# Four graph layers in one kernel: layer 0's second attention pass with the decoder's work placed between the next part's blocks, and its last 20 keys held in three copies

## The chip, the cores and the metric

The program runs on one core of one Trainium2 chip, as one launch that computes all four layers. The metric is the time on the device in microseconds (us); smaller is better. The core has five engines that work side by side, each in the order of its own queue: TensorE (PE in the profile; its weight loads are listed as PEld), VectorE (DVE), ScalarE (ACT), GpSimd (POOL) and SyncE (SP). They wait for each other by semaphores. SBUF is the memory on the chip, with 128 partitions; PSUM holds the sums of TensorE in 8 banks of 512 float32 columns for each partition.

## The reference

There are N = 2708 nodes with 512 features, and one 0/1 adjacency `adj` of 2708 x 2708 (about 1.2% of it is set). Layer 0 is the one the change touches. It is called with `adj` as the local and as the long-range pattern, so that its two softmaxes are the same one.

```python
H, D = 4, 128
Xh = X.reshape(n, H, D).transpose(1, 0, 2)
Xw = jnp.einsum('hnd,hde->hne', Xh, W)
f1 = jnp.einsum('hnd,hd->hn', Xw, V[:, 0, :, 0])
f2 = jnp.einsum('hnd,hd->hn', Xw, V[:, 1, :, 0])
sig = jax.nn.sigmoid(f1[:, :, None] + f2[:, None, :])
att = _masked_softmax(adj[None] * sig, (adj != 0)[None])
Xa = jnp.einsum('hij,hjd->hid', att, Xw)
Xc = Xa.transpose(1, 0, 2).reshape(n, F)
Xn = _batchnorm(Xc, enc_bn_gamma, enc_bn_beta)
emb = _mlp_block(Xn, enc_mlp_W, ...)          # batchnorm(elu(x @ Wm.T + bm) + x)
Yh = emb.reshape(n, H, D).transpose(1, 0, 2)
Y = jnp.einsum('hij,hjd->hid', att, Yh)       # the second pass
Y = jnp.einsum('hnd,hed->hne', Y, W)          # the decoder: w0T
Yc = jax.nn.elu(Y.transpose(1, 0, 2).reshape(n, F))
out = _mlp_block(Yc, dec_mlp_W, ...)          # dec_w, elu, + x, batchnorm
```

The layer's output is added to its input and normalised by rows. Layers 1 to 3 (a mean over neighbours, and two softmax layers over all pairs) follow; the change leaves them as they are.

## The kernel before

Everything is float32. Layer 0 works on transposed data: features on the partitions, nodes along the columns. It runs over the keys twice. The first pass (`attention_pass(xw, True, ..., keep)`) gives `Xa` and the softmax's sums, the second (`attention_pass(emb, False, ..., decode)`) gives `Y` with the same weights, which are computed again.

A pass has four parts: the queries in two halves of 1354 (`hf`), and for each half two pairs of heads (`p`). A part runs over 22 blocks of keys (`BLOCKS`): 21 of 128 and a last one of 20, since 2708 = 21 x 128 + 20. For each block `form` makes a tile `t` of weights, 128 keys x (2 heads x 1354 queries): SP loads a stripe `a` of the adjacency (L300), ACT takes tanh for each of the two heads (L313), DVE multiplies with the stripe (L321), ACT takes exp of both (L322). Four tiles `t` go round. Some blocks' tiles (`KEPT`) are written to DRAM in the first pass and loaded back in the second. In the first pass's parts with `p` = 0 the stripe is first prepared by DVE (L303, L304) and written to DRAM for later (L307, POOL). L284 counts neighbours for layer 1.

TensorE then multiplies the tile with the block's values (L366): two heads x three chunks of 452, 452 and 450 queries (`HCH`), six products a block, added up over all 22 blocks in six PSUM banks `po` (three tiles `both[q]` of two banks). Of the last block, the products have 20 rows. In the first pass there are also the softmax's sums (L389, four 32-column products side by side).

When a part is through, `finish` is called. In the first pass it is `keep`: it copies the six banks to `ft` (L466), computes a small product once (`ps_beta`, L434), and returns the scaling by the sums as a list `later`, of which one entry is done with every block after the fourth (`jt > 3`). In the second pass it is `decode`, which does its whole work at once. It reads the six banks with scaling (L660, into `ot`), and for each of the six chunks adds a shift where a node has neighbours (L672), multiplies with w0T (`ps_y`, L676) and takes elu (L403 on ACT, L406 and L408 on DVE). After the second pair of heads of a half follows the decoder's mlp: for each of three chunks and four output blocks, four products with `dec_w` (`ps_dec`, L687), elu (L405 on ACT), the addition to `ot` (L705) and statistics for the batch normalisation (L706). `ps_y` and `ps_dec` share two more banks (`misc`).

After the second pass, layer 1's weights are loaded and centred (L735, L737), the statistics are put together (L418) and inverted (`inv_std`: L92, a square root on ACT at L93, L94), and layer 1 starts with scaling `ot` (L774), adding the input (L781) and transposing (L787) and multiplying (L113) each block of nodes. The order of instructions in each engine's queue is fixed when the program is built, by a scheduler that follows the order of the code where it can.

Of the kernel before, what the change touches and what calls it, by code (L numbers as in the profile page):

```python
# [17 lines left out]
P = 128  # L18
# [11 lines left out]
def gnn_stack_kernel(  # L30
# [32 lines left out]
    BANK = 512  # L63

# [86 lines left out]
    with ExitStack() as l0:  # L151
# [20 lines left out]
        f2h = p0.tile([P, NT, H], F32, name="f2h")  # L172

# [12 lines left out]
        def project(att, psum):  # L186
# [41 lines left out]
            for jt, (j0, n) in enumerate(BLOCKS):  # L228
                pxw = psum.tile([P, H // HP, BANK], F32, tag=f"po{jt % HB}", name="pxw")
                pv = pxw[:, :, : HP * (P + 2)].rearrange("p a (k e) -> p a k e", k=HP)  # L230
                for h in range(H):
                    nc.tensor.matmul(
                        pv[:n, h // HP, h % HP, :],
                        xT_sb[:, h, j0 : j0 + n],
                        w0x[:, h, :],
                        start=True,
                        stop=True,
                    )
                copy = nc.vector.tensor_copy if jt % 3 == 2 else nc.scalar.copy
                copy(  # L240
                    xw[:n, jt, :].rearrange("p (a k d) -> p a k d", a=H // HP, k=HP),
                    pv[:n, :, :, :P],
                )
                nc.vector.tensor_scalar(
                    f2h[:n, jt, :].rearrange("p (a k) -> p a k", k=HP),
                    pv[:n, :, :, P + 1],
                    0.5,
                    None,
                    ALU.mult,
                )  # L250
            return f1b
# [18 lines left out]
        def attention_pass(values, first, att, psum, finish, f1b=None):  # L270
# [23 lines left out]
            def form(hf, p, jt, att, prepare, f1b, tv):  # L294
# [5 lines left out]
                nc.sync.dma_start(a[:n, :w], src[j0 : j0 + n, h0 : h0 + w])  # L300
                if prepare:
# [5 lines left out]
                    nc.gpsimd.dma_start(adj_d[j0 : j0 + n, h0 : h0 + w], a[:n, :w])  # L307
# [16 lines left out]
            later = []  # L324
            for hf, (h0, w) in enumerate(HSPAN):
                for p in range(H // HP):
                    prepare = first and p == 0
                    if f1b is None or not prepare or hf > 0:
# [6 lines left out]
                    both = [  # L335
                        psum.tile([P, HP, BANK], F32, tag=f"po{q}", name="po", bufs=1)
                        for q in range(HB)
                    ]
                    po = [both[q][:, k, :] for k in range(HP) for q in range(HB)]
# [7 lines left out]
                    for jt, (j0, n) in enumerate(BLOCKS):  # L347


                        if jt > 3 and later:  # L350
                            later.pop(0)()
# [3 lines left out]
                        if kept is None or first:  # L355
                            form(hf, p, jt, att, prepare, f1b, tv)
                            if kept is not None:
                                nc.gpsimd.dma_start(kept[:n, :, :w], tv)
                        else:
                            nc.sync.dma_start(tv, kept[:n, :, :w])  # L360
                            if p == 0 and jt in KEPT[1]:
                                count(hf, jt, att)
                        for k in range(HP):
                            h = HP * p + k
                            for q, (q0, qw) in enumerate(HCH[hf]):
                                nc.tensor.matmul(  # L366
                                    po[HB * k + q][:, :qw],
                                    values[:n, jt, h * P : (h + 1) * P],
                                    t[:n, k, q0 : q0 + qw],
                                    start=(jt == 0),  # L370
                                    stop=(jt == NT - 1),
                                )
# [23 lines left out]
                    later += finish(hf, p, po, sums if first else rb) or []  # L396

        def elu(pool, ps, w, bias=None, less=-1.0, dst=None):
# [5 lines left out]
            else:  # L404
                nc.scalar.activation(m, ps, AF.Exp, bias=bias)  # L405
            nc.vector.tensor_scalar(r, ps, less, -1.0, ALU.add, ALU.max)  # L406
# [39 lines left out]
        with (  # L446
# [7 lines left out]
            def keep(hf, p, po, sums):  # L454
# [3 lines left out]
                elif hf == 0 and p == 1:  # L458
                    ps = psum.tile([P, HP, BANK], F32, tag="po0", name="ps_beta")[:, 0, :C]
                    small_product(ps, mlp_w[0], prm_sb[:, B_ENC, :])  # L460
                    nc.vector.tensor_tensor(bias[:, 0, :], ps, prm_sb[:, MB_ENC, :], ALU.add)
                final = hf == NHALF - 1 and p == H // HP - 1
                for k in range(HP):
                    for q, (q0, qw) in enumerate(HCH[hf]):
# [3 lines left out]
                        )  # L468
                sm = [att.tile([P, BW], F32, tag="rs", name="sm") for _ in range(HP)]
# [86 lines left out]
        with (  # L556
# [36 lines left out]
            for ci, (c0, w) in enumerate(CHUNKS):  # L593
# [34 lines left out]
                while turned < NT and sum(BLOCKS[turned]) <= c0 + w:  # L628
# [5 lines left out]
                    turned += 1  # L634

# [8 lines left out]
            links = {}  # L644

            def decode(hf, p, po, rb):
# [10 lines left out]
                for k in range(HP):  # L657
                    h = HP * p + k
                    for q, (q0, qw) in enumerate(HCH[hf]):
                        nc.vector.scalar_tensor_tensor(  # L660
                            t[:, h, q0 : q0 + qw],
                            po[HB * k + q][:, :qw],
                            scale2[:, h : h + 1],
                            rb[:, k, q0 : q0 + qw],
                            ALU.mult,
                            ALU.mult,
                        )
                for k in range(HP):
                    h = HP * p + k
                    for q, (q0, qw) in enumerate(HCH[hf]):  # L670
                        y = t[:, h, q0 : q0 + qw]
                        nc.vector.scalar_tensor_tensor(  # L672
                            y, y, shift2[:, h : h + 1], linked[:, q0 : q0 + qw], ALU.add, ALU.mult
                        )
                        ps = psum.tile([P, BANK], F32, tag="misc", name="ps_y", bufs=2)
                        nc.tensor.matmul(  # L676
                            ps[:, :qw], w0T_sb[:, h, :], y, start=True, stop=True
                        )
                        elu(att, ps[:, :qw], qw, dst=y)
                if p + 1 < H // HP:  # L680
                    return
                for q, (q0, qw) in enumerate(HCH[hf]):
                    rs = []
                    for o in range(C):
                        ps = psum.tile([P, BANK], F32, tag="misc", name="ps_dec", bufs=2)
                        for c in range(C):
                            nc.tensor.matmul(  # L687
                                ps[:, :qw],
                                dec_w[:, c, o * P : (o + 1) * P],
                                t[:, c, q0 : q0 + qw],  # L690
                                start=(c == 0),
                                stop=(c == C - 1),
                            )
                        rs.append(
                            elu(
                                att,
                                ps[:, :qw],
                                qw,
                                prm_sb[:, MB_DEC, o : o + 1],
                                bm1[:, o : o + 1],  # L700
                            )
                        )
                    for o in range(C):
                        dst = t[:, o, q0 : q0 + qw]
                        nc.vector.tensor_tensor(dst, dst, rs[o], ALU.add)  # L705
                        nc.vector.bn_stats(stats[:, o, HB * hf + q, :], dst)  # L706

# [164 lines left out]


    Q = 32
    REST = N - NFULL * P
    assert 0 < REST <= Q and C * Q == P
# [538 lines left out]
```

## Time and profile before

The median of three timed runs is 3387.1 us (3385.58 to 3390.83). The profiled execution took 3383.28 us; the span from its first to its last instruction is 3381.5 us.

| stretch, us from the span's start | what runs |
|---|---|
| 0 to 592 | projections and the first pass; parts end at about 183, 312, 457 and 584 |
| 592 to 703 | weights of a later layer, the encoder's mlp |
| 703 to 1181 | the second pass; parts end at about 812, 921, 1074 and 1181 |
| 921 to 974 | the decoder's mlp of the first half, with first blocks of the third part |
| 1181 to 1231 | the decoder of the last part |
| 1231 to 1244 | until layer 1's first transpose |
| 1244 to 3381 | layers 1 to 3 |

| group | count | mean ns of one |
|---|---|---|
| L313 ACT, tanh of one head | 324 | 1414 |
| L322 ACT, exp of both heads | 162 | 2452 |
| L321 DVE, product with the stripe | 162 | 2975 |
| L366 PE, 128 keys x 452 queries (second pass) | 672 | 556 |
| L366 PE, 20 keys x 452 queries (second pass) | 32 | 550 |

How to read it: a float32 matmul stands in the profile as two records. Matmuls overlap their neighbours, so the mean of one is longer than the step from one to the next. The rows of the windows view give, for each engine, busy time and (xN) the number of its records, then the granted TensorE clock, the share of the DMA engines and GB/s. Square brackets in a timeline give idle time before a row, and what ended it.

### The profile page before, as it was taken

How to read it: one execution, taken by the hardware profiler on the slowest of the kernel's cores; microseconds unless marked ns; L12 is line 12 of the kernel's file. 1: busy time of each engine (PE TensorE's matmuls, PEld its weight loads, DVE VectorE, ACT ScalarE, POOL GpSimd, SP SyncE). 2: the span in 40 equal slices, each digit the busy share in tenths (PEclk: the TensorE clock that was granted, in tenths of full speed). 3: DMA queues.
4: the chain of work that ended last, by engine and by line, in shares of the span. 5: the costliest groups of instructions: out<-in, count | busy, mean ns of one | idle time of the engine just before them, and what ended most of it. 6: DMA issues, size and time to landing. Idle time of an engine off the chain costs nothing.

```text
span 3381.5 us, 30504 instructions
## 1 busy us (share of the span) xinstructions
PE 3304.0 (98%) x10981; PEld 1761.1 (52%) x10981; DVE 1988.8 (59%) x3227; ACT 1339.6 (40%) x1491; POOL 127.6 (4%) x205
## 2 busy tenths in 40 slices
PE   8999999999999989999999999999999999999998
PEld 4444444544444445886555555444455555555554
DVE  7867977767687585445136666777253442543533
ACT  6877887568858743001133333333011010110110
POOL 1100100000000000000010000000000000000001
PEclk9998999999999999999999999999999999999999
DMA  7655753335524331550034444554111111111100
GB/s 279 246 164 166 276 184 114 120 103 168 184 82 160 126 106 61 140 136 19 0 114 125 116 127 128 145 148 112 58 50 35 44 33 44 37 33 44 35 23 19
DMA packets 167483, 364.03 MB, mean 108 GB/s; under 512 B 20374, under 2 KB 111194, under 8 KB 164100
## 3 DMA queue, kind: packets, MB, share of 16 engines
q1 hardware_dynamic: 152596, 298.43, 29.3%
q0 software_dynamic: 14736, 63.66, 5.0%
q8 instruction: 86, 1.41, 0.2%
q14 instruction: 65, 0.53, 0.0%
HBM read 298.34 MB, written 63.35 MB: 107 GB/s over the span
## 4 chain that ended last, share of the span: by engine, by line
PE 74%; issue 15%; DVE 6%; DMA 2%; ACT 2%; POOL 1%; SPq 0%; POOLq 0%; DVEq 0%; ACTq 0%
PE po L1090 22%; PE ps_s L996 17%; PE po L366 8%; PE ps_nb L842 7%; PE ps_wide L908 4%; PE ps_hid L113 2%; PE ps_sup L1233 2%; DVE t L321 2%; PE ps_o L1168 2%; PE ps_dec L687 2%; PE ps_mlp L601 1%; DMA a<-adj_d 1%; POOL adj_d L307 1%; PE ps_s L991 1%; ACT t L313 1%
## 5 line engine op out<-in xcount | busy, mean ns | idle before, releaser
L321 DVE SCALAR_TENSOR_TENSOR t<-t,a 128x2708 f32<-128x2708 f32 (+1 forms) x162 | 479.3, 2975 | 144.8 <-ACT t L313 143.3
L313 ACT ACTIVATE t<-f1b,f2h 128x1354 f32<-128x1354 f32 (+1 forms) x324 | 445.3, 1414 | 91.2 <-PE psm L389 47.1
L366 PE MATMUL po<-t,xw 128*128 128x452 f32 (+3 forms) x1056 | 433.0, 561 | 3.9 <-ACT t L322 3.9
L366 PE MATMUL po<-t,emb 128*128 128x452 f32 (+3 forms) x1056 | 416.3, 552 | 10.7 <-ACT t L322 9.2
L322 ACT ACTIVATE t<-t 128x2708 f32<-128x2708 f32 (+1 forms) x162 | 396.7, 2452 | 52.0 <-DVE t L321 50.5
L1090 PE MATMUL po<-sup,e 128*128 128x512 f32 x882 | 410.0, 601 | 5.2 <-DVE e L1277 5.2
L1090 PE MATMUL po<-e,xs 128*128 128x384 f32 (+1 forms) x1176 | 407.5, 489 | 0.0
L996 PE MATMUL ps_s<-q,hT 128*128 128x384 f32 (+1 forms) x1176 | 403.5, 489 | 0.0
L1331 DVE SCALAR_TENSOR_TENSOR e<-a_cols,ps_s 128x384 f32<-128x384 f32 (+1 forms) x154 | 85.6, 556 | 419.7 <-PE ps_s L996 396.6
L366 PEld LDWEIGHTS po<-t,emb 128*128 128x128 f32 (+1 forms) x1056 | 201.6, 193 | 220.1 <-issue 199.2
L366 PEld LDWEIGHTS po<-t,xw 128*128 128x128 f32 (+1 forms) x1056 | 197.8, 193 | 224.9 <-issue 211.4
L996 PEld LDWEIGHTS ps_s<-q,hT 128*128 128x128 f32 x1176 | 222.6, 190 | 161.5 <-issue 6.2
L1090 PEld LDWEIGHTS po<-e,xs 128*128 128x128 f32 x1176 | 221.6, 190 | 157.2 <-issue 6.0
L1090 PEld LDWEIGHTS po<-sup,e 128*128 128x128 f32 x882 | 162.0, 192 | 176.8 <-issue 148.3
L996 PE MATMUL ps_s<-hT 128*128 128x384 f32 (+1 forms) x672 | 229.2, 488 | 1.0 <-ACT sup L1240 0.7
L93 ACT ACTIVATE ln_rstd<-ln_rstd 128x1 f32<-128x1 f32 x88 | 17.2, 201 | 497.4 <-DVE ln_rstd L92 496.9
L1273 ACT ACTIVATE a_cols<-a_cols,neg_big 128x384 f32<-128x384 f32 (+1 forms) x154 | 94.8, 616 | 249.7 <-DMA a_cols<-in_adjT_dram 208.4
L842 PE MATMUL ps_nb<-hid_hi,at 128*128 128x512 f32 x484 | 188.1, 390 | 0.4 <-DVE at L836 0.4
L842 PE MATMUL ps_nb<-hid_lo,at 128*128 128x512 f32 x484 | 187.8, 389 | 0.0
L1067 ACT COPY nmax<-pb 128x384 f32<-128x384 f32 (+1 forms) x14 | 6.7, 479 | 430.5 <-PE pb L1054 349.8
L996 PEld LDWEIGHTS ps_s<-hT 128*128 128x128 f32 x672 | 125.8, 190 | 97.1 <-issue 18.0
L1085 DVE TENSOR_TENSOR acc<-acc,e 128x384 f32<-128x384 f32 (+2 forms) x294 | 162.9, 554 | 12.3 <-ACT e L1075 2.3
(223 smaller groups left out, 3474.1 us busy)
## 6 DMA issues: line engine op xcount, KB each, us to landing
a<-adj_d SPq DMA_DIRECT2D x116, 677.0 KB
a_cols<-in_adjT_dram SPq DMA_DIRECT2D x378, 192.0 KB
a<-in_adjT_dram SPq DMA_DIRECT2D x42, 677.0 KB
adj_d<-a POOLq DMA_DIRECT2D x42, 677.0 KB, 4.5
raw<-in_adjT_dram SPq DMA_DIRECT2D x105, 256.0 KB
kept<-t POOLq DMA_DIRECT2D x10, 1354.0 KB, 6.6
t<-kept SPq DMA_DIRECT2D x10, 1354.0 KB
a_cols<-in_adjT_dram SPq DMA_DIRECT2D x63, 202.0 KB
```

Source lines behind the costliest of these rows:

```text
L113: nc.tensor.matmul(ps[:n], xt[:, c, :n], w[:, c, :], start=(c == 0), stop=(c == C - 1))
L313: nc.scalar.activation(tv[:, k, :], f1b[:n, k, :w], AF.Tanh, bias=f2h[:n, jt, h : h + 1], scale=0.5,)
L321: nc.vector.scalar_tensor_tensor(tv, tv, GUARD, ab, ALU.add, ALU.mult)
L322: nc.scalar.activation(tv, tv, AF.Exp, scale=0.5)
L366: nc.tensor.matmul(po[HB * k + q][:, :qw], values[:n, jt, h * P : (h + 1) * P], t[:n, k, q0 : q0 + qw], start=(jt == 0), stop=(jt == NT - 1),)
L842: nc.tensor.matmul(pos[it], at, half[:, jt, :], start=(jt == 0 and k == 0), stop=(jt == NT - 1 and k == 1),)
L908: nc.tensor.matmul(ps[:, :width], w(c, o), xt(c), start=(c == 0), stop=(c == C - 1),)
L996: nc.tensor.matmul(ps[:, :w], keys[:, c, j0 : j0 + P], st["q"][:, c, :], start=(c == 0), stop=(c == C - 1),)
L1085: nc.vector.tensor_tensor(acc, acc, e[:m], ALU.add)
L1090: nc.tensor.matmul(out, lhsT, rhs, start=(k == 0), stop=(k == NT - 1))
L1273: nc.scalar.activation(a, a, AF.Identity, bias=neg_big[: a.shape[0]], scale=1.0e30)
L1331: nc.vector.scalar_tensor_tensor(e, a, 2.0, ps, ALU.mult, ALU.add)
```

## The change

Three things, all in layer 0.

*Twenty keys in three copies.* The values of the last block, and f2 of its nodes, are copied by POOL to the rows 32 to 51 and 64 to 83 (`copies`). The last block's stripe `a` is loaded three times, to rows 0, 32 and 64; the 12 rows between are filled from other rows of the adjacency. `form` works on 84 rows (`HR`), and the products of chunk q take the rows from 32 q. Kept tiles are loaded three times.

*Banks.* The six banks are allocated once for each pass instead of for each part; `ps_beta` uses the first of them, after the copies.

*The decoder.* `decode` still reads the six banks when a part ends. Shift, product with w0T and elu of each chunk (`after`), and the mlp of the chunks 0 and 1 of the first half, are returned as a list; one entry is done with every block from the second on. The mlp of the first half's chunk 2 is kept in `spare` and done behind the last block of the second pass, where the last part's work is written out by chunk. There (`wide`) the mlp's result goes to a tile `r` of its own, so that it can be added and its statistics taken at once; ACT copies three of four back. A square root of one column (`ready`) comes before the last statistics.

```diff
+        def copies(rows):
+            for r in range(1, HB):
+                nc.gpsimd.dma_start(rows[r * Q : r * Q + REST], rows[:REST])
...
+            copies(xw[:, NT - 1, :])
+            copies(f2h[:, NT - 1, :])
...
                 nc.sync.dma_start(a[:n, :w], src[j0 : j0 + n, h0 : h0 + w])
+                if n < P:
+                    for r in range(HB):
+                        if r > 0:
+                            nc.sync.dma_start(
+                                a[r * Q : r * Q + n, :w], src[j0 : j0 + n, h0 : h0 + w]
+                            )
+                        if r + 1 < HB:
+                            nc.sync.dma_start(
+                                a[r * Q + n : (r + 1) * Q, :w], src[: Q - n, h0 : h0 + w]
+                            )
+                    n = HR
...
-                        if jt > 3 and later:
+                        if jt > (3 if first else 0) and later:
                             later.pop(0)()
...
-                            nc.sync.dma_start(tv, kept[:n, :, :w])
+                            for r in range(0, P if n == P else HB * Q, P if n == P else Q):
+                                nc.sync.dma_start(t[r : r + n, :, :w], kept[:n, :, :w])
...
                             for q, (q0, qw) in enumerate(HCH[hf]):
+                                r = 0 if n == P else q * Q
                                 nc.tensor.matmul(
                                     po[HB * k + q][:, :qw],
-                                    values[:n, jt, h * P : (h + 1) * P],
-                                    t[:n, k, q0 : q0 + qw],
+                                    values[r : r + n, jt, h * P : (h + 1) * P],
+                                    t[r : r + n, k, q0 : q0 + qw],
...
+            if last:
+                ready = small.tile([P, 1], F32, tag="ready", name="ready")
+                nc.scalar.activation(ready, m[:, 0:1], AF.Sqrt)
...
+                def after(k, q):
+                    shifted(k, q)
+                    turn(k, q)
+
+                if not final:
+                    for k in range(HP):
+                        for q in range(HB):
+                            take(k, q)
+                    rest = [lambda k=k, q=q: after(k, q) for k in range(HP) for q in range(HB)]
+                    for q in range(HB if last else 0):
+                        st = {}
+                        wide = q + 1 == HB
+                        dest = spare if wide else rest
+                        dest += [
+                            lambda q=q, o=o, st=st, wide=wide: mlp(q, o, st, wide) for o in range(C)
+                        ]
+                    return rest
+
+                def begin(q):
+                    for k in range(HP):
+                        take(k, q)
+                    for k in range(HP):
+                        shifted(k, q)
+
+                def turns(q):
+                    for k in range(HP):
+                        turn(k, q)
+
+                begin(0)
+                spare[0]()
+                turns(0)
+                spare[1]()
+                begin(1)
+                spare[2]()
+                spare[3]()
+                for q in range(HB):
+                    st = {}
+                    mlp(q, 0, st, True)
+                    mlp(q, 1, st, True)
+                    if q + 1 < HB:
+                        turns(q + 1)
+                    if q + 2 < HB:
+                        begin(q + 2)
+                    mlp(q, 2, st, True)
+                    mlp(q, 3, st, True)
```

`take` is the read of one bank (the old L660), `shifted` the old L672, `turn` the old L676 with its elu. `mlp(q, o, st, wide)` holds the four products and the elu of one output block:

```python
                def mlp(q, o, st, wide):
                    ...
                    r = None
                    if wide:
                        if o == 0:
                            st["r"] = att.tile([P, HP, HW], F32, tag="t", name="r_dec", bufs=4)
                        r = st["r"].rearrange("p k w -> p (k w)")[:, o * BW : o * BW + qw]
                    r = elu(att, ps[:, :qw], qw, ..., dst=r, last=final and q + 1 == HB and o + 1 == C)
                    st.setdefault("sums", []).append((t[:, o, q0 : q0 + qw], r, o))

                    def add(dst, y, r, o):
                        nc.vector.tensor_tensor(dst, y, r, ALU.add)
                        nc.vector.bn_stats(stats[:, o, HB * hf + q, :], dst)

                    if wide and o + 1 < C:
                        y, r, o = st["sums"][-1]
                        add(r, y, r, o)
                    elif o + 1 == C:
                        for y, r, o in st["sums"]:
                            if wide and o + 1 < C:
                                nc.scalar.copy(y, r)
                            else:
                                add(y, y, r, o)
```

## The prediction, made before the changed kernel was run

> **What bounds the kernel now.** I read the page first, then the stretch that the change touches part by part, then single instructions. All times are of the profiled execution: 3383.3 us, span 3381.5.
>
> ```profile
> PE 3304.0 (98%) x10981; PEld 1761.1 (52%) x10981; DVE 1988.8 (59%) x3227; ACT 1339.6 (40%) x1491; POOL 127.6 (4%) x205
> PEclk9998999999999999999999999999999999999999
> PE 74%; issue 15%; DVE 6%; DMA 2%; ACT 2%; POOL 1%; SPq 0%; POOLq 0%; DVEq 0%; ACTq 0%
> ```
>
> TensorE sets the time, so an edit is worth what it takes from TensorE's queue or from TensorE's waits. A busy PE is not PE at its peak, however. The chain of waits, in order of time, has one undisturbed stretch:
>
> ```profile
> 828.08 77.62 PE po L366 x204
> ```
>
> 77.62 / 204 = 0.38 us is one record of 452 columns at full clock; each float32 matmul makes two. Below, records x 0.38 is "work", and the rest of a stretch is "excess". The two passes over the keys end at about 592 and 1181 us; each has four parts (two halves of the queries, two pairs of heads). The second pass, cut where a part's last matmul ends:
>
> ```profile
> core 0: us, PE busy (x) PEld busy (x) DVE busy (x) ACT busy (x) POOL busy (x), PEclk, DMA share, GB/s
> 812.50:921.60 109.10, 107.27 (x277) 52.63 (x276) 74.99 (x54) 95.81 (x62) 0.00 (x0) 0.98 0.54 179
> 921.60:974.00 52.40, 51.09 (x128) 24.80 (x129) 48.91 (x71) 21.94 (x24) 0.00 (x0) 0.97 0.30 101
> 974.00:1074.90 100.90, 95.84 (x246) 46.31 (x244) 74.48 (x57) 84.78 (x52) 0.00 (x0) 0.98 0.39 123
> 1074.90:1181.60 106.70, 106.66 (x276) 52.73 (x276) 63.96 (x47) 81.35 (x53) 0.00 (x0) 0.98 0.42 142
> 1181.60:1231.00 49.40, 44.06 (x109) 20.71 (x109) 35.85 (x62) 10.28 (x17) 0.00 (x0) 0.94 0.32 115
> 1231.00:1244.00 13.00, 3.60 (x9) 1.36 (x8) 11.97 (x30) 3.69 (x6) 0.00 (x0) 0.81 0.58 184
> ```
>
> Excess, row by row: 109.1 - 277 x 0.38 = 3.8; 52.4 - 48.6 = 3.8; 100.9 - 93.5 = 7.4; 106.7 - 104.9 = 1.8; 49.4 - 41.4 = 8.0. The last row is the wait for the batch statistics: TensorE leaves its last decoder product at 1231.0 and starts layer 1 at 1244.0. In row 2 VectorE is busy 48.91 of 52.40 us.
>
> **1. Twenty keys in three copies.** Groups by shape, and the same kind of product later in the kernel, where 20-row matmuls already sit in different row groups:
>
> ```profile
> L366 PE MATMUL po<-t,emb 20*128 20x452 f32 x32 | 13.8, 550 | 0.0
> 2013.62 1.13 PE L1090 MATMUL po<-values,e 20*128 20x512 f32 x6
> ```
>
> Now a 20-key block is 12 records in single file, 12 x 0.38 = 4.57 us. At L1090 six records of 512 columns take 1.07 us to the next start (2013.62 to 2014.69): three run at once, in two rounds. The changed block is two such groups of 452 columns: 2 x 1.07 x 452/512 = 1.9 us. Saved: 2.7 us x 8 blocks = **21.3 us**. Bounds: 0 (no overlap) to 8 x (4.57 - 4 x 0.38) = 24.4.
>
> [...]
>
> What it adds elsewhere: ACT and DVE work on 84 rows for 20, at no cost, since the time goes by columns: the 20-row L321 at 572.08 us took 2.97, the mean of the group is 2975 ns. SP issues four more loads at the end of each of the first pass's parts, two more in the second's; at 0.5 us (three L300 issues took 1.50) that is 2 us of SP per part, with the next part's first loads queued behind. The four `a` buffers of the first pass hide it; uncovered it would be 8 us. POOL issues six more copies, 0.57 us each (an L507 issue) and 3.4 in all, with `adj_d` writes behind them that are read a part later: nothing.
>
> **2. What the short block uncovers.** The six reads of the sums were under the 4.57 us:
>
> ```profile
> 811.10 3.66 DVE L660 SCALAR_TENSOR_TENSOR ot<-po,bn_scale,rb 128x452 f32<-128x452 f32 x6 [1.26 <-PE po L366]
> 814.68 3.08 DVE L672 SCALAR_TENSOR_TENSOR ot<-ot,bn_shift,linked 128x452 f32<-128x452 f32 x5
> 822.57 2.97 DVE L321 SCALAR_TENSOR_TENSOR t<-t,a 128x2708 f32<-128x2708 f32 x1
> ```
>
> Two reads (2 x 0.6, and 0.2 of signalling) must be done before the next part's first product; before, TensorE waited 0.1 there. So 1.4 us at each of the three inner ends of each pass: 8.4. In the second pass DVE now does one shift, then an L321, then the second shift, and TensorE's queue has both `ps_y` products after the part's first block. From the block's end DVE needs 3.7 (six reads) + 0.6 + 3.0 + 0.6 = 7.9 us, TensorE 1.4 + 4.57 + 0.76 = 6.7: a wait of 1.1, three times, with all later `po` products behind it. Given back: **11.7 us**. Bounds: 0 (banks free one by one as they are summed) to twice that. Allocating the banks once adds no instruction; I give it nothing.
>
> **3. Decoder work spread out.** 48 products of dec_w per half and 6 `ps_y` per part stay. Half 0's 12 x 4 products no longer stand at the part's start: 8 x 4 go between blocks of the third part, 4 x 4 behind the last block. VectorE still does for a part's six turns 6 x (0.6 + 1.15) = 10.5 us, and per dec step about 2.3 us (0.6 + 0.54 + 0.54 + 0.6) under 3.04 of products. In the third part: 19 L321 (56) + 20 L284 (31, at 1.55) + reads 4.2 + 10.5 + 8 x 2.3 = 120 us. TensorE has 21 blocks of 4.57 and one of 1.9, the six turns and 32 products: 97.9 + 4.6 + 24.3 = 127. That is tight, so of row 3's 7.4 I take back only 2.9. Of row 2's 3.8, 1.7 is clock (below), 2.1 goes. Behind the last block the four held-back steps cover reads and shifts: of 8.0 I take 6, leaving 2. **11.0 us.** Bounds: 0 to 17.
>
> **4. The tail.** After the last product, before: 13.0 us. Now three of four sums and statistics come earlier, the square root's table load (1.28) moves before them. Remaining on VectorE: 0.9 until its first, 0.7 + 0.6 + 0.6 + 0.6, statistics 0.3, the four L737 still in between (2.4), then about 4.8 of small steps, L767 (1.16), L774 and L781: 10.9. **2.1 us**; bounds 0 to 4.5 (L737 elsewhere). Twelve ACT copies of 0.6 lie beside it: ACT is 10.28 of 49.4 us busy.
>
> **5. The clock.** Part ends show half clock:
>
> ```profile
> 181.00:191.00 10.00, 10.00 (x27) 3.56 (x26) 7.79 (x8) 6.76 (x7) 1.17 (x2) 0.50 0.11 13
> 454.00:464.00 10.00, 10.00 (x27) 3.65 (x26) 7.32 (x8) 8.19 (x6) 1.17 (x2) 0.50 0.46 143
> 1075.00:1079.00 4.00, 4.00 (x7) 1.81 (x8) 4.00 (x8) 0.11 (x1) 0.00 (x0) 0.57 0.99 360
> 909.00:913.00 4.00, 2.88 (x9) 1.20 (x8) 2.80 (x2) 4.00 (x3) 0.00 (x0) 1.00 0.77 213
> ```
>
> In these (first three) TensorE is busy throughout, just behind 20-row products; a real gap (the fourth, 1.1 us idle) left the clock alone. Similar stretches at all eight ends but the last add up to about 51 us at half speed (10.2, 17.1, 10.2, 3.4 in pass one; three of 3.4 in pass two), 25.6 us lost. The new block is 1.9 us at 60 rows, plus 1.4 us of waiting: that is shorter, yet a 2.15 us gap at 751.1 us was also followed by half clock. And the 17 us stretch has 32 one-column products (L434) that stay; ACT's 22 x 5.3 = 116 us per part in pass one leaves little under TensorE's 119. I take **10 us**; bounds 0 and 25.6.
>
> [...]
>
> **Sum.** 21.3 - 11.7 + 11.0 + 2.1 + 10 = 32.7; 3383.3 - 32.7 = 3350.6. The median shown (3387.1) is 3.8 above the profiled run, so 3354.
>
> **Rivals.**
> - *All half-clock stretches go.* For it: they start within 4.1 us of the 20-row products. Against: L434, the 1.4 us waits. 15.6 more: 3338.
> - *The three copies do not overlap at L366* (separate waits of the second and third product on their copies' DMAs). For: each new copy has its own semaphore. Against: L1090. Term 1 and term 5 go, and 8.4 of term 2 with them: 3354 + 31.3 - 8.4 = 3377.
> - *TensorE waits on VectorE at each inserted step, and the kernel is slower.* 26 inserted steps in parts two to four (6, 6 + 8, 6) stand in TensorE's queue; if VectorE is within an L321 (2.97) when each is due, and the formed tiles run out behind it, up to 77 us. For: 120 of 127 us in part three. Against: parts two and four have VectorE at 64 to 75 us of 107. It decides from (32.7 + 3.3) / 26 = 1.4 us a step; at 2 us: 3354 + 52 - 3.3 = 3403.
>
> **How the numbers follow.** Forecast 0.55, its own range 3342 to 3366; full clock 0.22; no overlap 0.13; slower 0.07; about nothing 0.03. The range 3332 to 3378 reaches from the second case past the third. Faster by more than 0.2% (6.8 us, about what a measurement can tell) 0.90, within 0.03, slower 0.07.
>
> **What would show it.** Six L366 20-row records starting within 0.5 us in threes; L660 to first product of a part about 1.4 us; `ps_y` steps with waits near 1 us; no dec_w block at a part's start; last dec_w to first layer-1 transpose about 11 us; clock 0.5 stretches shorter. Wrong if these 20-row starts are 0.38 apart, or if the third part's steps wait over 1.4 us each.

## The result, and the profile after

The changed kernel took 3358.8 us (median of four runs, 3358.7 to 3363.6), the kernel before 3386.3 beside it (3383.9 to 3390.8): ratio 0.9921, 95% interval 0.9905 to 0.9937, or 27.5 us less. The forecast was 3354 (0.9902 of the 3387.1 it started from), its range 3332 to 3378. The profiled run of after is the slowest of the four: 3363.6 us, span 3361.8, so the two profiles differ by 19.7 us only, and that is what the sums below account for. The page of after, its engines, clock and the shares of the chain of waits:

```profile
PE 3272.6 (97%) x10981; PEld 1751.3 (52%) x10981; DVE 1991.5 (59%) x3228; ACT 1344.1 (40%) x1504; POOL 130.0 (4%) x211
PEclk9999999999999999999999999999999999999999
PE 73%; issue 13%; DVE 7%; DMA 3%; ACT 3%; POOL 1%; SPq 0%; POOLq 0%; DVEq 0%; ACTq 0%
```

TensorE still sets the time, with as many records and 31.4 us less of busy time. The windows view of after, first by stage (first pass; between the passes; second pass until layer 1's first transpose; layers 1 to 3), then the second pass where a part's last matmul waits are over:

```profile
core 0: us, PE busy (x) PEld busy (x) DVE busy (x) ACT busy (x) POOL busy (x), PEclk, DMA share, GB/s
0.00:585.70 585.70, 561.80 (x2532) 261.95 (x2532) 468.22 (x351) 465.89 (x299) 43.65 (x82) 0.98 0.61 209
585.70:693.70 108.00, 107.09 (x356) 57.84 (x357) 78.62 (x116) 47.78 (x60) 3.01 (x4) 0.95 0.27 94
693.70:1227.30 533.60, 503.83 (x1326) 246.60 (x1324) 392.62 (x380) 396.25 (x286) 1.06 (x2) 0.97 0.45 148
1227.30:3361.80 2134.50, 2099.89 (x6769) 1184.93 (x6769) 1052.01 (x2384) 434.16 (x860) 82.34 (x123) 0.99 0.26 73
...
803.00:915.80 112.80, 106.04 (x277) 51.56 (x277) 76.90 (x53) 96.44 (x62) 0.00 (x0) 0.96 0.58 191
915.80:1052.50 136.70, 131.04 (x340) 64.39 (x341) 114.84 (x112) 100.69 (x71) 0.00 (x0) 0.96 0.41 132
1052.50:1156.90 104.40, 104.38 (x276) 51.73 (x276) 63.33 (x45) 84.07 (x54) 0.00 (x0) 0.98 0.46 152
1156.90:1216.20 59.30, 55.64 (x144) 27.13 (x142) 51.48 (x86) 18.81 (x33) 0.00 (x0) 0.97 0.27 96
1216.20:1227.30 11.10, 3.56 (x9) 1.29 (x7) 10.30 (x24) 4.28 (x8) 0.00 (x0) 0.88 0.50 151
```

The first three stages of before, for the same cuts:

```profile
0.00:598.70 598.70, 582.33 (x2532) 268.92 (x2533) 468.76 (x350) 466.20 (x299) 41.86 (x78) 0.97 0.58 202
598.70:702.60 103.90, 102.58 (x355) 54.89 (x356) 78.31 (x116) 47.80 (x60) 3.00 (x4) 1.00 0.28 97
702.60:1244.00 541.40, 514.73 (x1326) 250.50 (x1325) 388.80 (x380) 391.30 (x273) 0.00 (x0) 0.97 0.43 144
```

So the first pass gained 13.0 us, the second 7.8, and the stretch between them, whose code is the same, lost 4.1; layers 1 to 3, whose code is the same too, differ by 3.0 (in the runs of this study they take 2133.4 to 2138.3 us, with 28 to 32 us at half clock in the shorter ones and 37 to 39 in the longer; before has 38.3, after 28.4). The length of a stage minus TensorE's busy time is TensorE's idle time: 16.4 us in the first pass before and 23.9 after, 26.7 and 29.8 in the second. The gain is all in busy time, part of it given back in waits.

The decoder has moved as announced: no row holds a block of `dec_w` products of its own, the third part has 340 records in one row, and the stretch behind the last block has 144 records for 109.

### The profile page after: what moved, and what is told of

Same layout as the page of the kernel before. It is cut to its first block, busy times and chain, and to the rows that moved or that the text cites. A ratio compares the mean times of both kernels' runs of the same rounds, so it can differ in the third digit from the quotient of the medians.

```text
span 3361.8 us, 30553 instructions
## 1 busy us (share of the span) xinstructions
PE 3272.6 (97%) x10981; PEld 1751.3 (52%) x10981; DVE 1991.5 (59%) x3228; ACT 1344.1 (40%) x1504; POOL 130.0 (4%) x211
## 4 chain that ended last, share of the span: by engine, by line
PE 73%; issue 13%; DVE 7%; DMA 3%; ACT 3%; POOL 1%; SPq 0%; POOLq 0%; DVEq 0%; ACTq 0%
PE po L1195 22%; PE ps_s L1101 17%; PE po L397 8%; PE ps_nb L952 7%; PE ps_wide L1013 4%; DVE t L349 3%; PE ps_hid L118 2%; PE ps_sup L1338 2%; PE ps_o L1273 2%; PE ps_mlp L637 2%; DMA a<-adj_d 1%; ACT t L341 1%; DMA a_cols<-in_adjT_dram 1%; PE ps_dec L733 1%; ACT t L350 1%
## 5 line engine op out<-in xcount | busy, mean ns | idle before, releaser
L349 DVE SCALAR_TENSOR_TENSOR t<-t,a 128x2708 f32<-128x2708 f32 (+1 forms) x162 | 480.0, 2974 | 146.6 <-ACT t L341 144.8
L397 PE MATMUL po<-t,emb 128*128 128x452 f32 (+3 forms) x1056 | 408.3, 556 | 17.9 <-ACT t L350 10.1
L397 PE MATMUL po<-t,xw 128*128 128x452 f32 (+3 forms) x1056 | 415.8, 557 | 9.0 <-ACT ft L499 4.8
L397 PEld LDWEIGHTS po<-t,emb 128*128 128x128 f32 (+1 forms) x1056 | 197.2, 194 | 222.3 <-issue 197.3
L397 PEld LDWEIGHTS po<-t,xw 128*128 128x128 f32 (+1 forms) x1056 | 191.0, 192 | 221.0 <-issue 202.5
```

Source lines behind the costliest of these rows:

```text
L349: nc.vector.scalar_tensor_tensor(tv, tv, GUARD, ab, ALU.add, ALU.mult)
L397: nc.tensor.matmul(po[HB * k + q][:, :qw], values[r : r + n, jt, h * P : (h + 1) * P], t[r : r + n, k, q0 : q0 + qw], start=(jt == 0), sto ...
```

## The experiments

Of every run below I use three numbers besides the ratio: TensorE's busy and idle time in the two passes, from the stage rows, and the time at half clock, from the trace's record of the granted clock (its stretches are 3.4 us or small multiples: before layer 1, up to 17.1 us in before and 13.7 in after). Half of that time is lost where TensorE has work: full rows, below, take out 61.3 us of it in the passes and 30.4 us of busy time. The sums below add stretches rounded to 0.1 us. The second pass's always hold one stretch that has nothing to do with the short block, in TensorE's long wait for the batch statistics in the tail: 10.2 us in before, the copies alone, both kernels with padding alone and the short block in the middle, 6.8 in the others. The line of the products is L366 before, L397 after, L393 in the copies alone and L372 where full rows are the only edit.

**The copies alone.** Before, with the first part of the diff only (and not the banks):

```diff
+            copies(xw[:, NT - 1, :])
+            copies(f2h[:, NT - 1, :])
...
+                                r = 0 if n == P else q * Q
...
-                                    values[:n, jt, h * P : (h + 1) * P],
-                                    t[:n, k, q0 : q0 + qw],
+                                    values[r : r + n, jt, h * P : (h + 1) * P],
+                                    t[r : r + n, k, q0 : q0 + qw],
```

> The kernel before with the three copies of the last 20 keys alone, in both passes; decoder and banks as before. Theory A (the parts of the change eat each other): the short block saves 2.85 us at each of 8 ends, but in the second pass the reads of the sums then stand in the open, so that most of the gain is that of the first pass (13.0 us until its end in the traces) and about 3 at the very end: 3367 to 3374, gain 12 to 19. Theory B (the parts add up): the full 21 to 23 us, 3363 to 3365.

Measured: 3380.2 us (ten runs) against 3378.6 before (thirteen), 0.9999 (0.9990 to 1.0009). No gain, which was in neither expectation. The stages of the copies alone:

```profile
0.00:586.20 586.20, 561.81 (x2532) 261.76 (x2533) 468.28 (x351) 465.70 (x299) 44.08 (x82) 0.98 0.59 209
586.20:694.20 108.00, 107.13 (x356) 57.75 (x357) 78.60 (x116) 47.78 (x60) 3.00 (x4) 0.95 0.26 94
694.20:1243.70 549.50, 505.26 (x1326) 244.40 (x1325) 387.90 (x380) 392.15 (x273) 1.06 (x2) 0.97 0.43 145
```

TensorE is busy for 1067.1 us in the passes instead of 1097.1: 22.8 of the difference are the shorter blocks (below), 5.1 the clock, at half for 64.7 us in place of 74.9. But its idle time rose from 16.4 to 24.4 and from 26.7 to 44.2: 25.5 us of waits. With the 4.1 lost between the passes the gain is used up. Where the waits are, from the timeline of TensorE at the third part's end:

```profile
1066.09 1.79 PE L393 MATMUL po<-t,emb 20*128 20x452 f32 x12
1069.85 1.02 PE L704 MATMUL ps_y<-ot,w0T_sb 128*128 128x452 f32 x2 [1.96 <-DVE ot L700]
...
1079.30 1.02 PE L704 MATMUL ps_y<-ot,w0T_sb 128*128 128x450 f32 x2 [0.64 <-DVE elu_r L433]
1084.68 1.88 PE L393 MATMUL po<-t,emb 128*128 128x452 f32 x2 [4.35 <-ACT t L346]
```

Here the decoder's six turns still come in one piece when a part ends. The short block lets TensorE reach them sooner, VectorE needs as long as ever, and the next tile's multiplication stands behind its turns: the 4.35 us end with a tile `t`. The wait has moved, with its length, from under the old block to behind it.

**The decoder alone.** After without the copies: `copies` and the fill of `a` are left out, and

```diff
-                            rows = n if n == P else HR
+                            rows = n
...
-                                r = 0 if n == P else q * Q
+                                r = 0
```

> The changed kernel without the three copies: the last block again has 20 rows in single file; decoder and banks as changed. Theory A: third part and end as in the changed kernel (4.0 and 7.2 us less), the reads covered again by 4.6 us, no 3.3 us wait at a part's start: gain 11 to 16, 3370 to 3375. Theory B: what is left of 27.5 when 21 to 23 are the copies': gain 4 to 7, 3379 to 3382.

Measured: 3368.0 us, 0.9955 (0.9940 to 0.9970), 15 us by the ratio; against the median of all thirteen runs of before it is 10.6. Its second pass:

```profile
704.40:1232.40 528.00, 512.97 (x1326) 251.72 (x1324) 392.61 (x380) 396.21 (x286) 0.00 (x0) 0.97 0.43 146
```

Idle time is 15.0 us instead of 26.7. Most of the change's gain is here.

**Full rows for the last block.** The third question was whether 20 rows or the gaps behind them halve the clock. Before, with no copies and nothing moved, but the last block's products done on 128 rows: the values of rows 20 to 127 are zero, and the other rows of the stripe are filled from the adjacency, so that every weight is finite. The sums are the same.

```diff
+            nc.vector.memset(xw[:, NT - 1, :], 0.0)
+            nc.vector.memset(emb[:, NT - 1, :], 0.0)
...
+                if n < P:
+                    nc.sync.dma_start(a[n:P, :w], src[: P - n, h0 : h0 + w])
...
-                                    values[:n, jt, h * P : (h + 1) * P],
-                                    t[:n, k, q0 : q0 + qw],
+                                    values[:, jt, h * P : (h + 1) * P],
+                                    t[:, k, q0 : q0 + qw],
```

> The kernel before, with the last block's products on all 128 rows: its values have zeros in the rows 20 to 127, its tile is formed on 128 rows. As many records as before, of the same length. Theory C (the clock is halved because 20 of 128 rows work): no half clock at the ends of the parts except where the one-column products stand and at the very end, 35 to 45 us of half clock less, 10 to 20 us faster than before: 3366 to 3376. Theory D (the halving comes from the change of part, its waits and reads): the same stretches, 3384 to 3388.

Measured: 3358.3 us, 0.9924 (0.9909 to 0.9939): these few lines are worth as much as the whole change, and more than the 10 to 20 us expected. The stages, and the first part's last block in the timeline:

```profile
0.00:579.50 579.50, 562.49 (x2533) 260.96 (x2533) 468.65 (x352) 467.03 (x299) 42.01 (x78) 1.00 0.63 221
579.50:684.80 105.30, 103.62 (x355) 55.84 (x356) 78.53 (x117) 48.22 (x60) 3.00 (x4) 0.98 0.27 96
684.80:1215.30 530.50, 504.22 (x1326) 247.97 (x1325) 388.37 (x380) 391.06 (x273) 0.00 (x0) 0.99 0.45 155
...
176.58 4.82 PE L372 MATMUL po<-t,xw 128*128 128x452 f32 x12
```

The same block of before, in its timeline:

```profile
177.35 5.89 PE L366 MATMUL po<-t,xw 20*128 20x452 f32 x12
```

Half clock in the passes falls from 74.9 us (40.9 and 34.0) to 13.6 (none in the first), half of which is 30.7; busy time falls by 30.4. Idle time stays, 17.0 and 26.3 us: the long block is still there to hide the reads. That settles it for the first pass of before: its 40.9 us at half clock, with TensorE busy for all of them, came with the 20-row products, and with rows of zeros added none is left. Of the 13.6 us left in the second pass, 10.2 are the tail's.

**64 rows.** The same with `values[: max(n, 64), ...]` and `t[: max(n, 64), ...]`.

> The kernel before with the last block's products on 64 rows (44 of them zeros), as many records as before and as long. If the clock follows the number of rows at work, half of them lies between: theory C1, 64 rows are enough to keep the clock and the time is that of 128 rows (3356 to 3362); theory C2, half of the rows are still too few and the stretches at the ends stay (3378 to 3387, 35 us or more of half clock in the first pass).

Measured: 3362.2 us, 0.9933 (0.9915 to 0.9951), not told apart from 128 rows by its interval. Half clock is 3.4 us in the first pass, where 20 rows had 40.9. So 64 rows are enough there. In the second it is 20.4: 10.2 in the tail, and 3.4 and 6.8 that begin during or just after waits of 1.99 and 2.83 us.

**The short block in the middle.** After, with the keys in the order 0 to 9, 20, 21, 10 to 19, so that a full block ends each part:

```diff
+            ORDER = list(range(10)) + [NT - 2, NT - 1] + list(range(10, NT - 2))
...
-                    for jt, (j0, n) in enumerate(BLOCKS):
+                    for at, jt in enumerate(ORDER):
+                        n = BLOCKS[jt][1]
...
-                                    start=(jt == 0),
-                                    stop=(jt == NT - 1),
+                                    start=(at == 0),
+                                    stop=(at == NT - 1),
```

> The changed kernel with the blocks of a part in another order: 0 to 9, then 20 and the short 21, then 10 to 19, so that a full block is last. Theory A: the six reads lie beside the full last block's products again, the short block saves its 2.85 us in the middle and leaves the clock alone: the 7.8 us of waits at the second pass's inner ends and some 6 at the first's go down to 2 to 4 together, and some of the clock comes back: 8 to 18 us faster than the changed kernel, 3341 to 3351. Theory E (the reads are late because VectorE's queue has its long products ahead of them wherever the short block stands): no gain, 3356 to 3361.

Measured: 3352.6 us, 0.9910 (0.9894 to 0.9927), between the two expectations. The waits stayed: 25.6 us idle in the first pass, and in the second, by its row,

```profile
685.40:1209.40 524.00, 496.94 (x1327) 243.94 (x1325) 392.13 (x380) 396.02 (x286) 1.05 (x2) 0.98 0.45 151
```

27.1, where after has 23.9 and 29.8. The timeline shows why: the block that now comes last has a tile made on the spot, not one loaded back, and VectorE is at two multiplications for the next part until TensorE is through.

```profile
786.27 5.87 DVE L349 SCALAR_TENSOR_TENSOR t<-t,a 128x2708 f32<-128x2708 f32 x2 [4.09 <-ACT t L341]
792.05 3.65 DVE L702 SCALAR_TENSOR_TENSOR ot<-po,bn_scale,rb 128x452 f32<-128x452 f32 x6
794.66 1.68 PE L397 MATMUL po<-t,emb 128*128 128x452 f32 x2 [2.68 <-DVE ot L702]
```

So a full last block is not enough where VectorE itself is late. What this order did gain was clock: 34.0 us at half in the passes for 64.7 in after, a saving of 15.3, and busy time is 14.5 lower. In the second pass a short block inside full work has no wait beside it, and the clock stays full; the first of them is at 743.36:

```profile
743.40:753.40 10.00, 10.00 (x35) 4.93 (x35) 8.95 (x7) 8.81 (x6) 0.00 (x0) 1.00 0.83 322
```

Outside the tail 23.8 us of half clock are left, in seven stretches. Six of them begin during, or at most 1.2 us after, a wait of 1.9 to 4.6 us between full blocks, the seventh behind products of one column.

**Decoder and full rows together.** The decoder's part of the change, with the padding in place of the copies.

> The changed kernel with the three copies taken out and the last block's products on 128 rows with zeros instead (the edits of e2 and e3 together). Theory C (the copies' gain was the clock's, and the full rows get it without uncovering the reads): the gains of the two add up, 15 and 20 us: 3341 to 3350 beside a before of 3379 to 3386, 8 to 15 us faster than the changed kernel. Theory F (both e2 and e3 remove the same waits and half clock at the parts' ends): no better than e3 alone, 3356 to 3362.

Measured: 3342.0 us against 3385.4, 0.9875 (0.9861 to 0.9890). On the same chip the changed kernel took 3362.5, so padding beats copying by 20.5 us. The passes:

```profile
0.00:580.90 580.90, 562.26 (x2533) 260.98 (x2533) 468.71 (x352) 467.17 (x299) 41.89 (x78) 1.00 0.62 220
...
689.20:1207.80 518.60, 502.13 (x1327) 248.70 (x1325) 392.37 (x380) 396.11 (x286) 0.00 (x0) 0.99 0.46 158
```

Busy time, 1064.4 us, is that of after (1065.6) by the other way: half clock is 10.2 us (6.8 of it in the tail) in place of 64.7, no short block. Idle time is 18.6 and 16.5 us for 23.9 and 29.8. The two gains add, because they are of different kinds: the one takes out half clock, the other takes out waits.

**The changed kernel again,** beside it.

> The changed kernel once more, for a comparison on the same chip: 0.991 to 0.994 of the time before. If the half clock of 10.2 us during the one-column products between the passes belongs to where they fell in time and not to the change, it need not be there in this profile, and the time is 3 to 5 us less than in the first one (3363.6); if it belongs to the change, it is there again.

Measured: 3362.5 us (3360.4 to 3364.7), 0.9936 (0.9922 to 0.9951), or 22 us less than before by the ratio. With the first comparison, the two intervals together put the change at 16 to 32 us. Half clock in its profile is 54.5 us in the passes and again 10.2 between them.

**Banks for each part.** The kernel with decoder and full rows, the six banks allocated inside the part's loop, as before the change.

> The kernel of e5 (decoder as changed, last block on 128 rows) with the six banks allocated anew for each part, as before the change. My step gave the allocation nothing: within 3 us of e5 (3339 to 3346). If banks reused one by one matter, the next part's first products wait for whole tiles: 1 to 2 us at each of six inner ends, 6 to 12 us slower than e5.

Measured: 3340.7 us, 0.9879 (0.9864 to 0.9894), the same as with one allocation. The banks are worth nothing that can be measured: TensorE's idle time in the two passes is 32.7 us, with one allocation 35.1.

**Nothing held back.** The same kernel, with all of the first half's mlp between the third part's blocks (`wide = False`, `dest = rest`, and no `spare` calls).

> The kernel of e5 with all twelve mlp steps of the first half between the third part's blocks, none held back for the end. If the four held-back steps cover the reads and shifts of the last part (I counted 6 us for that), TensorE waits 3 to 6 us more between the last block and the first decoder products and the time is 3 to 8 us more than e5's. If VectorE is the limit behind the last block anyway, moving four steps (about 2.3 us of VectorE each) forward gives it room there: the same time or less than e5's.

Measured: 3341.5 us, 0.9880 (0.9861 to 0.9898), the same again. Behind the last block it leaves 4.3 us over its work (45.3 us for 108 records of 0.38), with the held-back steps 2.9 (56.1 for 140); in the whole second pass TensorE is idle for 17.4 us, with the held-back steps for 16.5. The times can't tell these apart.

## Why the prediction was right, and where it was not

The time and the sign were right; the make-up of the sum was not. Two terms were wrong by 10 and 12 us, both in the direction of too much gain. That the time still came within 5 us of the forecast is in part luck: gains that were not forecast, and scatter between runs.

**Term 1, three copies: right (forecast 21.3).** The groups by shape and the timeline of after:

```profile
L397 PE MATMUL po<-t,emb 20*128 20x452 f32 x32 | 7.1, 564 | 0.0
...
174.82 1.79 PE L397 MATMUL po<-t,xw 20*128 20x452 f32 x12
```

Three products run at once. The block takes 1.72 us from its first start to the next product (174.82 to 176.54) in place of 4.57: 8 x 2.85 = 22.8 us of TensorE's queue. The rival in which the copies do not overlap (3377) is out: the 1.72 us are 0.2 over four bare rounds of 0.38.

**Term 2, what the short block uncovers: mis-sized, 23.7 for 11.7.** Idle time of the two passes is 53.7 us in after and 30.0 with the decoder's part alone; the difference is the copies'. The step that failed is that the reads start when the block ends and that nothing else is late. The timeline of after at the second part's end:

```profile
910.88 2.98 DVE L349 SCALAR_TENSOR_TENSOR t<-t,a 128x2708 f32<-128x2708 f32 x1 [4.49 <-ACT t L341]
911.54 0.92 PE L397 MATMUL po<-t,emb 20*128 20x452 f32 x6
...
913.78 3.65 DVE L702 SCALAR_TENSOR_TENSOR ot<-po,bn_scale,rb 128x452 f32<-128x452 f32 x6
...
915.80 4.86 PE L397 MATMUL po<-t,emb 128*128 128x452 f32 x6 [3.34 <-DVE ot L702]
917.35 1.28 DVE L715 SCALAR_TENSOR_TENSOR ot<-ot,bn_shift,linked 128x452 f32<-128x452 f32 x2
```

The short block's products are over at about 912.5, but VectorE is in a multiplication (L349) until 913.9 that it began while they ran; TensorE waits 3.34 us for two reads, not 1.4. I had put an L321 between the two shifts, behind the reads, and left out the one ahead of them. The waits after the short block in the second pass are 1.46, 3.34 and 2.98 us (7.8 for 4.2); at the first of these ends VectorE was free, and there the 1.4 held. In the first pass they are 1.76, 1.22 and 3.07 (6.1 for 4.2), and 2.7 at its last end, which I had not counted. Two of these end with ACT's share of the reads, and the 1.22 and 1.4 of the 2.7 with something I had left out, VectorE's addition of the last block's tile for the softmax's sums (L414, 2.96 us), which the old block had covered too:

```profile
303.13 2.50 PE L420 MATMUL psm<-t,ones 128*32 128x340 f32 x16 [1.22 <-DVE t L414]
...
447.26 2.63 PE L397 MATMUL po<-t,xw 128*128 128x452 f32 x3 [3.07 <-ACT ft L499]
```

The second-shift wait is 0.7 us, in the second part only (its `ps_y`); 1.9 us more just behind it end with a tile `t`: 2.6 for 3.3. All these make 19.2 of the 23.7; of the rest 1.5 is behind the last block (a wait of 2.18 for 0.69).

**Terms 3 and 4, the decoder and the tail: nearly right (13.1 forecast).** The decoder alone takes 11.7 us of idle time out of the second pass (26.7 to 15.0). In the changed kernel, against the copies alone, it is 14.4 (44.2 to 29.8), since it also removes the waits that the copies had moved to the six turns. In the third part I had VectorE at 120 of 127 us and feared waits. It is busy for 114.8 of 136.7; that row is 10.4 us over its work (340 x 0.38 - 2.85 = 126.3), of which some 4 is clock (5.1 and 3.4 us at half while TensorE works), and 2.98 and 2.70 are two waits, the second with a counterpart of 2.03 before. No step of the decoder is among them. Behind the last block I left 2 us and after has 6.1 (59.3 for 140 records), the kernel with full rows 2.9. In the tail, from the last `dec_w` product to the first transpose, 13.4 became 11.6 us: 1.8 for 2.1, and as forecast the centring of layer 1's weights stayed between the statistics and the square root's last steps (timeline of after, VectorE):

```profile
1220.08 0.32 DVE L455 BATCH_NORM_AGGREGATE bn_mv<-stats_c 128x2 f32<-128x36 f32 x1
1220.45 2.48 DVE L847 SCALAR_TENSOR_TENSOR xs<-ps_w,xs 128x512 f32<-128x512 f32 x4
...
1224.05 1.21 DVE L877 COPY w_sb<-xs 128x2048 f32<-128x2048 f32 x1
```

**Term 5, the clock: wrong, 0 for 10.** Until layer 1, after spends 74.9 us at half clock, as before does. In the passes it fell from 74.9 to 64.7, between them it rose from 0 to 10.2. The reason I gave (half clock follows 20-row products at a busy TensorE) is right for the first pass of before, where 40.9 us at half clock became 3.4 on 64 rows and none on 128; the step that failed is that a shorter stretch of them, with 1.4 us of waiting, would be all there is. The waits became longer (term 2), and in after the half clock goes with them. Each of the ten stretches in its passes outside the tail begins during, or at most 1.4 us after, a wait of TensorE: of 1.2 to 3.1 us in the first pass, of 1.9 to 3.3 in the second. Two of those in the second pass stand beside no short block, and two short blocks there, with a wait of 1.46 us and with none in the next 4 us, kept the clock. The second pass of after, from each short block on:

```profile
799.70:809.70 10.00, 7.82 (x28) 3.48 (x28) 8.16 (x10) 5.97 (x5) 0.00 (x0) 1.00 0.87 284
910.70:920.70 10.00, 6.66 (x20) 3.11 (x20) 9.82 (x12) 7.97 (x6) 0.00 (x0) 0.67 0.71 245
1047.80:1057.80 10.00, 7.02 (x21) 3.25 (x21) 10.00 (x11) 7.55 (x5) 0.00 (x0) 0.66 0.79 282
1155.20:1161.20 6.00, 5.77 (x23) 2.51 (x22) 4.17 (x7) 0.83 (x2) 0.00 (x0) 1.00 0.47 131
```

So the block with its waits did little better in the first pass (27.3 us for 40.9) and no better in the second (30.6 for 23.8 outside the tail). With the short block in the middle of a part half clock fell to 34.0 us in both passes together, and what is left outside the tail stands at waits again, all but one stretch. This is read from where the stretches stand; no run took the waits away and kept the short block at the end.

**The sum.** 22.8 - 23.7 + 13.1 (idle time that went, both passes of the decoder alone) + 0 is 12.2 us. The profiles differ by 19.7: 3.0 of the rest is in layers 1 to 3, 1.0 between the passes beside the clock, and 3.5 is busy time in the passes that neither the copies (22.8) nor the clock (5.1) accounts for. That last piece I can't place. The forecast's 32.7 came near the 27.5 of the medians because the timed runs had a larger difference than the profiles; that is luck.

**The rivals.** Not all half-clock stretches went (3338): 64.7 of 74.9 us stayed in the passes. TensorE does not wait at the inserted steps (3403): 0.7 us at all 26 of them, 2.6 with the wait for a tile behind one, 0.1 us a step, where the turning point was 1.4. Its mechanism, VectorE within an L321 when TensorE needs it, is real, but it struck at the reads of the sums. What I had no rival for is a half of the change that is worth nothing by itself.

**Open.** A kernel that puts the reads of the sums ahead of the multiplication in VectorE's queue, which would test term 2 by itself, was not tried; nor was one that keeps the short block at the end and removes only the waits behind it, which would test directly that the half clock in after is the waits'. The best kernels of the study, at 0.9875 to 0.9880, still have 16 to 17 us of idle time in the second pass.

## What to carry to other kernels

When a loop ends in a remainder of few rows, try to fill it up with zero rows before making it faster: here that took a few edits, kept the clock (13.6 us at half in the passes for 74.9) and kept the cover for the reads that follow (43.3 us of idle time for 43.1). Shortening a block is worth only what the engine behind it is early by (here 22.8 us of shorter blocks brought 25.5 us of waits); read from that engine's queue what it is doing when the block ends, not only how long its reads take. Run the parts of a change alone: two parts that were each argued at 10 to 20 us were worth 0 and 15.

## What the runs showed of the hardware that was not expected

*Half clock came with products of few rows.* Float32 products on 20 of 128 rows, six after another (4.57 us), were followed by half clock at a TensorE that had no gap: 40.9 us in the first pass. On 64 rows it was 3.4 us, on 128 none, with zeros in the added rows.

*It came with short waits too.* In after, outside the tail, waits of 1.2 to 3.3 us had half clock in them or right behind them, with and without few rows. Not every such wait has: one of 1.46 us in after and one of 1.94 in the decoder alone (at 753.13) left the clock full.

*And, at times, with products of one column.* Between the passes, two sets of 16 products of 128 rows and one column (32 records each; L434 before, L471 after) stand between full ones, and the half clock there begins during such a set or behind it. The same code ran at full clock in before and not in after; windows from 603 to 617 us of before,

```profile
603.00:617.00 14.00, 14.00 (x58) 8.29 (x57) 7.43 (x7) 11.61 (x13) 1.76 (x3) 1.00 0.98 360
```

and of after:

```profile
603.00:617.00 14.00, 14.00 (x49) 9.04 (x49) 7.84 (x8) 6.18 (x4) 2.28 (x4) 0.64 0.52 175
```

TensorE is busy for all of both. It was 10.2 us of half clock in both profiles of after, in the copies alone, with 64 rows, with decoder and full rows, and with nothing held back; 13.6 in the decoder alone; 3.4 with full rows alone and with the short block in the middle; and none in before and with banks for each part. Which it is does not follow the edits. In the traces of before and of after all half-clock stretches begin on a grid of 3.41 us. What sets it off at these products was not shown: no run moved them on purpose.

*Runs differ by their clock.* The thirteen runs of before beside the copies alone took 3386.95 us at a mean clock of 0.981 to 3375.28 at 0.985. The four of after took 3363.6 at 0.985 and 3358.7 to 3358.9 at 0.988. Single runs of one kernel scatter by as much as one part of this change is worth, and much of it shows in the granted clock.
